# Two graph attention layers: V of layer 0 in two halves, second half of a step reordered, a PSUM copy split over two engines

## The chip, the cores and the metric

The kernel runs on one core of a Trainium2 chip. The metric is the device time of one execution in microseconds (us). Before the change it was 3313.61 us (median of 3 runs, 3313.41 to 3314.32). All runs told of here were in the fast state. PE is TensorE, DVE VectorE, ACT ScalarE, POOL GpSimd; PEld is TensorE's weight load.

## The reference, cut to what matters

`x` is 128 graphs of 128 nodes by 512 features, `adj` their masks. Two attention layers, each with a residual and a layer norm; all in float32.

```python
# layer 0: 4 heads of 64
sim = where(adj, (x@Wq)(x@Wk)^T / 8, -max)
x = layernorm(x + softmax(sim) @ (x@Wv) @ Wo + bo)
# layer 1: 8 heads of 64, its own layer norm first, the diagonal added to the mask
q, k, v = split((layernorm(x)*gamma + beta) @ w_qkv.T)
scores = where(adj | eye, q k^T / 8, -1e9)
x = layernorm(x + softmax(scores) @ v @ w_out.T + b_out)
```

## The kernel before

Graphs go in groups of two. The program is a pipeline written by hand: step `s` makes Q, K and V of layer 0 for group s, layer 0's attention for group s-1, layer 1's projections for group s-2 (seven half-size products instead of eight, `p("qk", i)` and `p("v", i)`) and layer 1's attention for group s-3. There are 67 steps (0 to 66); each has two halves, one for each graph of the group. The order of issue in the program is the order on each engine.

```python
def p(kind, *which, g=s - 2):
    for i in which:
        product(kind, g, i)
    if setup:                 # preparatory work: layer 1's weights, gamma and beta transposed (17 pieces),
        setup.pop(0)()        # then weight_sums: 16 subtractions on VectorE
k = 2 * s
scores(k); c(0); flush(); residual(0, k - 1); p("", g=-1); c(1); flush(); p("", g=-1)
normalised(k); residual(1, k - 1); p("v", 4, 3, g=s - 3); flush()
transposed(1, s - 2); probs_t(k); p("qk", 1, 2); attend(k); load(s + 2); p("", g=-1)
k += 1                        # the second half
scores(k)
p("qk", 6, 5)
flush()
residual(0, k - 1)
p("qk", 7)
c(2)                          # V of layer 0, both graphs: 16 matmul passes
flush()
normalised(k)
residual(1, k - 1)
p("qk", 4, 3)
flush()
probs_t(k)
p("v", 1, 2)
attend(k)
p("v", 6, 5, 7)
transposed(0, s + 1)
```

(The calls of the first half are set on fewer lines here.) What they do:

- `scores`: TensorE makes q k^T of both layers into two PSUM tiles (sc); GpSimd fills sm, VectorE copies the scores in under the mask and reduces the maxima; the exponentials (ScalarE) are put in a list, which `flush` issues.
- `normalised`: VectorE takes the reciprocal sums (rec), GpSimd multiplies: `sm = sm * rec`, 128x512 for layer 0, 128x1024 for layer 1.
- `probs_t`: TensorE transposes sm into PSUM (pt); ScalarE copies layer 0's, VectorE layer 1's (pT).
- `attend`: TensorE makes V^T P^T (av), ScalarE copies it (aT), and for layer 1 scales the layer norm's output (h); GpSimd adds the bias.
- `residual(l, ...)`: TensorE multiplies by the output weights (o), VectorE adds and takes the statistics (st, mv), GpSimd makes 1/std (ve, rstd); the norm itself (VectorE) goes on the list.

The PSUM tiles of scores, pt and av (two banks each) share two buffers; the other results share two one-bank buffers; layer 1's products have two accumulators, "a" and "f".

## Time and profile before

| | before |
|---|---|
| time, median | 3313.61 us |
| profile's span | 3310.9 us |
| TensorE busy | 99% |
| VectorE, ScalarE, GpSimd busy | 47%, 40%, 41% |
| a step, scores to scores | 50.81 us |

The page's first part gives busy time and share for each engine. The chain of waits goes back from the last instruction to what released each one; where it names TensorE all along, only that engine's own work and what interrupts it count. The lines themselves are in the prediction.

### The profile page before, as it was taken

The numbers are of one execution on the slowest core, as the hardware profiler recorded it, in microseconds if no ns is written. First come the engines' busy times: TensorE is split into PE (matmuls) and PEld (weight loads), VectorE is DVE, ScalarE is ACT, GpSimd is POOL, SyncE is SP. The second block draws the span as 40 slices with busy tenths as digits, with TensorE's granted clock in tenths as the row PEclk, the third lists the DMA queues.
The fourth block names the chain that finished last, engine by engine and source line by source line (L and its number), as shares of the span: only waits on it lengthen the run. The fifth ranks groups of instructions, "written<-read, shape, count | busy, mean of one in ns | idle before, by whom it ended". The sixth has DMA issues, their size and how long they took to land.

```text
span 3310.9 us, 56223 instructions
## 1 busy us (share of the span) xinstructions
PE 3261.8 (99%) x22337; PEld 2650.8 (80%) x22337; DVE 1560.4 (47%) x2840; ACT 1330.8 (40%) x4432; POOL 1354.6 (41%) x1799
## 2 busy tenths in 40 slices
PE   8999999999999999999999999999999999999997
PEld 6888788888888887888888878888888788888875
DVE  3444444444544454445444444454444444444453
ACT  3444334434444343344443433443444344434443
POOL 2434444344344444443444444434434444344343
PEclk9999999999999999999999999999999999999998
DMA  3000000000000000000000000000000000000000
GB/s 117 21 17 24 17 27 24 17 24 27 17 24 21 24 24 17 26 25 17 24 26 19 24 17 27 24 18 24 27 17 24 17 27 24 17 24 27 11 13 17
DMA packets 57976, 79.64 MB, mean 24 GB/s; under 512 B 20840, under 2 KB 22384, under 8 KB 57712
## 3 DMA queue, kind: packets, MB, share of 16 engines
q1 hardware_dynamic: 57712, 76.04, 7.1%
q8 instruction: 175, 2.87, 0.4%
q14 instruction: 89, 0.73, 0.1%
HBM read 42.47 MB, written 33.55 MB: 23 GB/s over the span
## 4 chain that ended last, share of the span: by engine, by line
PE 96%; ACT 2%; DVE 1%; POOL 1%; issue 0%; DMA 0%; SPq 0%; POOLq 0%; DVEq 0%; ACTq 0%
PE o L411 19%; PE qka L233 14%; PE p L283 14%; PE va L233 7%; PE qkf L233 7%; PE p L293 7%; PE av L388 6%; PE sc L322 5%; PE pt L366 5%; PE qkc L233 3%; PE xt L178 3%; PE vf L233 3%; PE vc L233 2%; ACT aT L393 2%; POOL sm L356 0%
## 5 line engine op out<-in xcount | busy, mean ns | idle before, releaser
L347 ACT ACTIVATE sm<-sm,nmax 128x128 f32<-128x128 f32 x1536 | 595.2, 389 | 471.7 <-DVE nmax L338 469.7
L411 PE MATMUL o<-wo,aT 128*128 128x512 f32 x1536 | 704.3, 595 | 0.7 <-ACT aT L393 0.7
L411 PEld LDWEIGHTS o<-wo,aT 128*128 128x128 f32 x1536 | 287.6, 191 | 258.8 <-issue 247.9
L424 POOL TENSOR_SCALAR ve<-mv 128x1 f32<-128x1 f32 x256 | 56.9, 222 | 1044.3 <-DVE mv L421 1044.0
L356 POOL TENSOR_TENSOR sm<-sm,rec 128x512 f32<-128x512 f32 (+1 forms) x256 | 370.9, 1470 | 254.0 <-DVE rec L355 251.4
L283 PE MATMUL p<-xT,w 128*128 128x256 f32 x2048 | 472.2, 384 | 2.3 <-ACT xT L180 1.2
L283 PEld LDWEIGHTS p<-xT,w 128*128 128x128 f32 x2048 | 385.3, 191 | 87.5 <-issue 28.7
L335 DVE COPY_PREDICATED sm<-m,sc 128x512 f32<-128x512 uint8 (+1 forms) x512 | 271.5, 583 | 319.1 <-POOL sm L333 255.7
L402 POOL TENSOR_TENSOR h<-h,bias 128x512 f32<-128x512 f32 x128 | 162.1, 1266 | 506.1 <-ACT h L401 506.1
L347 ACT ACTIVATION_READ_ACCUMULATOR sm<-sm,nmax 128x1 f32 x1536 | 286.6, 187 | 0.0
L233 PEld LDWEIGHTS qka<-xs,wsqk 128*128 128x128 f32 x2048 | 243.2, 191 | 38.1 <-issue 27.5
L233 PE MATMUL qka<-xs,wsqk 128*128 128x128 f32 x2048 | 256.0, 278 | 0.0
L233 PE MATMUL qkf<-xs,w 128*128 128x128 f32 x2048 | 249.6, 275 | 0.0
L338 DVE TENSOR_REDUCE nmax<-sm 128x4 f32<-128x512 f32 (+1 forms) x256 | 243.9, 953 | 8.8
L417 DVE TENSOR_TENSOR y<-o,h 128x512 f32<-128x512 f32 x128 | 88.3, 690 | 324.9 <-PE o L411 324.9
L322 PE MATMUL sc<-qk 64*128 64x128 f32 x3072 | 224.6, 286 | 15.6 <-ACT aT L393 15.6
L233 PEld LDWEIGHTS qkf<-xs,w 128*128 128x128 f32 x2048 | 239.0, 192 | 0.0
L293 PE MATMUL p<-w,xT 128*128 128x256 f32 x1024 | 231.7, 379 | 0.2 <-DVE h L417 0.2
L322 PEld LDWEIGHTS sc<-qk 64*128 64x128 f32 x3072 | 187.4, 188 | 50.7 <-ACT aT L393 27.5
L393 ACT COPY aT<-av 128x768 f32<-128x768 f32 (+2 forms) x132 | 102.9, 780 | 302.8 <-PE av L388 302.8
L293 PEld LDWEIGHTS p<-w,xT 128*128 128x128 f32 x1024 | 189.7, 190 | 23.6 <-DVE h L417 0.4
L366 PE MATMUL pt<-ident,sm 128*128 128x128 f32 x1536 | 190.9, 274 | 12.6 <-POOL sm L356 12.6
(86 smaller groups left out, 4775.6 us busy)
## 6 DMA issues: line engine op xcount, KB each, us to landing
x<-in_x_dram SPq DMA_DIRECT2D x64, 512.0 KB, 3.7
out_dram<-y SPq DMA_DIRECT2D x128, 256.0 KB, 2.1
w_qkv<-in_L_gnn_w_qkv_dram SPq DMA_DIRECT2D x12, 256.0 KB, 5.6
m<-in_adj_dram SPq DMA_DIRECT2D x64, 32.0 KB, 3.5
w_out<-in_L_gnn_w_out_dram SPq DMA_DIRECT2D x4, 256.0 KB, 4.2
w<-in_L_gnn_Wq_dram SPq DMA_DIRECT2D x1, 512.0 KB, 4.4
w<-in_L_gnn_Wk_dram SPq DMA_DIRECT2D x1, 512.0 KB, 6.2
w<-in_L_gnn_Wv_dram SPq DMA_DIRECT2D x1, 512.0 KB, 7.1
```

The lines of the kernel that those rows point to most:

```text
L233: nc.tensor.matmul(o, lhsT, rhs, start=first and n == 0, stop=n == len(todo) - 1, skip_group_check=True)
L283: nc.tensor.matmul(pm[:, (f % 2) * T:(f % 2 + 1) * T], W[l][:, c, f * P:(f + 1) * P], xT[:, c, :], start=(c == 0), stop=(c == KC - 1))
L293: nc.tensor.matmul(pm[:, (b - b0) * I:(b - b0 + 1) * I], xT[:, c, b * N:(b + 1) * N], W[l][:, c, 2 * I:3 * I], start=(c == 0), stop=(c == ...
L322: nc.tensor.matmul(ps[:, h % 2, h // 2, :], qk[r, h // 2, t], qk[r, H_ // 2 + h // 2, t], start=True, stop=True)
L335: nc.vector.copy_predicated(sm[:, s], mask[:, None, :].to_broadcast([P, K, N]), ps[:, s, :K, :])
L338: nc.vector.tensor_reduce(nmax, sm, AX.X, ALU.max, negate=True)
L347: nc.scalar.activation(sm[:, s, k, :], sm[:, s, k, :], AF.Exp, bias=nmax[:, s, k:k + 1], accum_out=total[:, s, k:k + 1])
L356: nc.gpsimd.tensor_tensor(sm, sm, rec[:, :, :, None].to_broadcast([P, 2, K, N]), op=ALU.mult)
L366: nc.tensor.transpose(pt[:, j, :], sm[:, j, :], ident)
L388: nc.tensor.matmul(pm[s * D:(s + 1) * D, at + kk * N:at + (kk + 1) * N], v[:, b, h * D:(h + 1) * D], pT[:, s * K + kk, :], start=True, sto ...
L393: nc.scalar.copy(aT[:, lo - base:hi - base], pm[:, lo:hi])
L411: nc.tensor.matmul(pm, aT[:, c * P:(c + 1) * P], WO[l][:, c, :], start=(c == 0), stop=(c == nk - 1))
```

## The change

Its intent: put TensorE work (half of V) between the second scores and the attention ahead of them, so that the scores don't wait for aT; spread layer 1's products more finely; and share the copy of layer 1's transposed probabilities between two engines.

```diff
         else:
-            per = 512 // I
-            b0 = (n - nq) * per
-            for b in range(b0, b0 + per):
-                for c in range(KC):
-                    nc.tensor.matmul(pm[:, (b - b0) * I:(b - b0 + 1) * I], ...
-            dst = V[l, g][:, b0:b0 + per, :]
+            b = n - nq
+            for c in range(KC):
+                nc.tensor.matmul(pm[:, :I], xT[:, c, b * N:(b + 1) * N], W[l][:, c, 2 * I:3 * I], ...
+            dst, src = V[l, g][:, b, :], pm[:, :I]
...
             else:
-                nc.vector.tensor_copy(pT, pt[:, :H_, :])
+                nc.scalar.copy(pT[:, :K], pt[:, :K, :])
+                nc.vector.tensor_copy(pT[:, K:], pt[:, K:, :])
...
         load(s + 2)
+        c(2)
         p("", g=-1)
...
         p("qk", 7)
-        c(2)
         flush()
+        residual(1, k - 1)
         normalised(k)
-        residual(1, k - 1)
-        p("qk", 4, 3)
+        p("qk", 4)
         flush()
+        p("qk", 3)
+        p("v", 1)
         probs_t(k)
-        p("v", 1, 2)
+        p("v", 2)
+        c(3)
         attend(k)
```

(cut at the "..." inside the calls and between the hunks)

More of the change, by code (lines that the diff above doesn't have):

```diff
@@ L288, in chunk @@
         else:
-            per = 512 // I
-            b0 = (n - nq) * per
-            for b in range(b0, b0 + per):
-                for c in range(KC):
-                    nc.tensor.matmul(pm[:, (b - b0) * I:(b - b0 + 1) * I],
-                                     xT[:, c, b * N:(b + 1) * N], W[l][:, c, 2 * I:3 * I],
-                                     start=(c == 0), stop=(c == KC - 1))
-            dst = V[l, g][:, b0:b0 + per, :]
-            src = pm.rearrange("p (b i) -> p b i", i=I)
+            b = n - nq
+            for c in range(KC):
+                nc.tensor.matmul(pm[:, :I], xT[:, c, b * N:(b + 1) * N], W[l][:, c, 2 * I:3 * I],
+                                 start=(c == 0), stop=(c == KC - 1))
+            dst, src = V[l, g][:, b, :], pm[:, :I]
         if (n + l) % 2:
```

## The prediction

> **What bounds the kernel now.** I read the page first (busy shares and the chain of waits), then that chain in order of time for a stretch in the middle, then the timelines of VectorE, GpSimd and ScalarE for the same stretch.
>
> ```profile
> span 3310.9 us, 56223 instructions
> PE 3261.8 (99%) x22337; PEld 2650.8 (80%) x22337; DVE 1560.4 (47%) x2840; ACT 1330.8 (40%) x4432; POOL 1354.6 (41%) x1799
> PE 96%; ACT 2%; DVE 1%; POOL 1%; issue 0%; DMA 0%; SPq 0%; POOLq 0%; DVEq 0%; ACTq 0%
> ```
>
> TensorE is busy for 99% and carries 96% of the chain; no other engine is over 47%. So only what stops TensorE counts. Here is one half of a step in the chain (start, length, what):
>
> ```profile
> 1535.80 1.49 PE av L388 x24
> 1537.28 0.02 issue
> 1537.30 0.81 ACT aT L393
> 1538.11 0.04 issue
> 1538.15 1.16 PE sc L322 x16
> 1539.32 1.98 PE qka L233 x16
> 1541.30 1.79 PE qkf L233 x16
> 1543.09 1.72 PE o L411 x4
> 1544.80 1.78 PE qka L233 x16
> 1546.59 3.46 PE p L293 x16
> 1550.04 3.43 PE o L411 x8
> 1553.48 1.78 PE qka L233 x16
> 1555.26 1.79 PE qkf L233 x16
> 1557.05 1.31 PE pt L366 x12
> 1558.36 0.87 PE va L233 x4
> ```
>
> A step takes 50.81 us (first scores at 1514.52 and again at 1565.33 in the chain), and in these two steps the only piece that is not TensorE's is the ScalarE copy aT. After the first half's attention (av) the scores of layer 1 need the PSUM buffer that av holds, so they wait for aT. From the end of av (1537.28) to the end of the scores (1539.32) is 2.04 us; in the first half, with work in between, the same 24 score matmuls take 1.54 us in the chain. **The stall is 0.50 us a step**, and the wait table has it 62 times ("PE sc <- ACT aT").
>
> The second thing to read is slack. The probabilities' transposes (pt) need GpSimd's multiplication by the reciprocal sums:
>
> ```profile
> 1551.46 2.89 POOL L356 TENSOR_TENSOR sm<-sm,rec 128x512 f32<-128x512 f32 x2 [3.11 <-DVE rec L355]
> 1555.24 0.22 POOL L424 TENSOR_SCALAR ve<-mv 128x1 f32<-128x1 f32 x1 [0.89 <-DVE mv L421]
> 1555.55 0.58 POOL L431 TENSOR_TENSOR rstd<-ve,mhalf 128x1 f32<-128x1 f32 x1
> 1556.10 1.27 POOL L402 TENSOR_TENSOR x<-x,bias 128x512 f32<-128x512 f32 x1
> ```
>
> The pair of multiplications (layer 0, then layer 1) ends at 1554.35 and pt runs from 1557.05: 2.7 us of slack, today. In the second half the order is: multiplications, then residual(1)'s variance and power (ve, rstd). The change swaps them.
>
> **What the Trainium skill says.** "TensorEngine Tiling (Array Packing)", Key Properties: changing the tiling mode drains TensorE. The trace agrees: scores use 64 rows and av 64 columns, and the product after each is 0.20 us longer than its like (in the chain p after sc 3.65 against 3.45, va after av 1.06 against 0.86). "TensorE: Matmul & The Clock Gate", the table at its top: ScalarE, VectorE and GpSimd are strict FIFO; the trace's order on each is the program's, so the swap above binds. "Advanced Engine Details and Errata", Bank Collisions: ScalarE and VectorE may read PSUM at once if their banks differ; the split copy of pT does that, and no trace of before has this pair to judge. "GPSIMD Engine Reference", Specifications: its SBUF interface is contended by VectorE instructions with two SBUF inputs. The x bias add is 1264 to 1707 ns by its line, median 1268, so lengthening is rare.
>
> **The change, part by part.**
>
> (a) V of layer 0, batch 0, moves between av and the second scores; batch 1 moves to just before the second av. The 16 matmuls (3.46 us) become 8 and 8, 1.73 each. The first 8 follow av directly, so they pay the switch: 1.93. They cover aT's 0.81 and the scores fall to 1.54. Sum before: 2.04 + 3.46 = 5.50. After: 1.93 + 1.54 + 1.73 = 5.20 (the switch into and out of the second av is there already). **Gain 0.30 us a step**: 0.50 of stall less 0.20 for one more switch. The evictions are one 128x512 VectorE copy (691 ns) replaced by a 128x256 on VectorE (about 424, the like-sized v adds) and one on ScalarE (about 372, the v copies); both beside TensorE work.
>
> (b) pT of layer 1: 1224 ns on VectorE become about 691 on VectorE and 586 on ScalarE in parallel. av waits for pT 2.8 us in the whole run, so nearly nothing is gained here: some 0.5 us for each of the last two half-steps, where the chain does run through this copy.
>
> (c) The second half's order. Between o (layer 1) and pt TensorE now has qk4, qk3 and one v product: 1.78 + 1.79 + 0.87 = 4.44 us (before 3.57). But the multiplications, which used to start during o, now follow residual(1), which needs o's end. Count from the first matmul of o (1549.88 in TensorE's timeline; the chain books it from 1550.04, the end of the piece before). VectorE's add started at 1553.52, 3.64 after; the statistics ended at 1555.15; ve started 5.36 after and GpSimd was free again at 1556.10, 6.22 after. These depend only on o, as VectorE's earlier queue (layer 0's norms) is done some 2 us after o starts. So the multiplications run from 6.22 to 6.22 + 2.89 = 9.11 (layer 0's 1040 ns end at 7.26, layer 1's 1897 ns at 9.11). TensorE without a wait: o ends 3.60 after (1553.48), and 4.44 more bring it to pt at 8.04; layer 0's four transposes are in time, and all twelve would end at 9.35. Layer 1's eight cannot start before 9.11 + 0.04; the chain shows once, near the end, what such a wait looks like:
>
> ```profile
> 3199.41 2.89 POOL sm L356 x2
> 3202.29 0.04 issue
> 3202.34 1.09 PE pt L366 x8
> ```
>
> So 0.04 from GpSimd's end, then 1.09 for the eight: they end at 9.11 + 0.04 + 1.09 = 10.24, against 9.35. **New stall 0.89 us a step**, which nothing later gives back: TensorE's order is fixed and it is the bound.
>
> Sum: +0.89 - 0.30 = +0.59 us a step. Both layers are present in 61 steps (3 to 63 of 0 to 66): +36.0. Step 64 has no V to fill in, so +0.9; step 65 has layer 1 alone, 8 transposes without the four ahead and one multiplication: about +0.4; the last step gains about 1.0 by (b); the three first steps pay the switch or lose nothing, +0.4. Together about +36.7: 3313.6 + 36.7 = **3350 us**.
>
> **Rivals.**
> - *The transposes don't stall*: then only (a) counts, 61 x -0.30 = -18, 3295 us. For it: the change was surely meant so, and first-half slack is large (multiplications end 2.8 us ahead of pt). Against it: the sums in (c) leave minus 0.8 us, and each is a duration in the trace.
> - *The stall is longer*: norms and multiplications now run on VectorE and GpSimd at once. GpSimd's tiny ratio op takes 340 to 606 ns, the longer ones beside VectorE's norms. Another 0.3 to 0.5 us on the multiplications would make +55 to +67, 3368 to 3381 us. But layer 1's multiplications have a mean of 1897 ns and a longest of 1900, although those of the second half already run beside VectorE's residual add.
> - *aT's wait is replaced, not removed*: the scores' masks wait for GpSimd's memset (VectorE idles 3.97 before it), which hangs on av's end and not on the scores. It moves 1.9 us towards the scores' start, so it only relaxes; a fresh PSUM wait for the half chunks is unlikely, since each evicted tile is over 1 us old when it is needed. If it held, (a) would give 0 and the time would be near 3369.
>
> **Range and chances.** The mechanism of (c) carries the sign. I give it about 85%. With it the stall is 0.7 to 1.2 us, so 3338 to 3369; without it about 3295. Range 3328 to 3370. Two per cent are 66 us: slower by more needs 1.1 us a step net, about twice the sum; 6%. Faster by over 2% would need all switches gone too; 1%.
>
> **What would show it.** In the changed chain: sc after the V half in 1.54 with no aT ahead of it (a); a POOL sm piece ahead of "PE pt x8" in every second half, of about 0.9 us, with the eight at 1.09 (c); in the wait table "PE pt <- POOL sm" some 62 times in place of "PE sc <- ACT aT"; GpSimd's rstd ahead of sm in the second half; a period of 51.4 us. I am wrong if pt runs x12 in 1.31 in the second half, or if the multiplications there start before ve.

## The result, and the profile after

The changed kernel took **3373.82 us** (4 runs, 3372.97 to 3374.29), beside 3313.97 for the kernel before: +59.9 us, ratio 1.018 (95% interval 1.0162 to 1.0197). A ratio is the mean time of one kernel's fast runs over that of the other's of the same rounds, so it isn't quite the ratio of the medians quoted. The predicted 3350 and its range to 3370 were too low.

The page of the changed kernel, the lines that answer to the first ones in the prediction:

```profile
span 3372.1 us, 56347 instructions
...
PE 3274.9 (97%) x22337; PEld 2638.5 (78%) x22337; DVE 1518.3 (45%) x2840; ACT 1423.6 (42%) x4624; POOL 1374.7 (41%) x1799
...
PE 86%; POOL 7%; DVE 4%; issue 1%; ACT 1%; DMA 0%; SPq 0%; POOLq 0%; DVEq 0%; ACTq 0%
```

TensorE's share of the chain fell from 96 to 86%, and GpSimd and VectorE came in with 7 and 4. The chain in order of time (start, length, what) shows where, in one half step of the middle:

```profile
1519.00 1.92 PE p L291 x8
1520.92 1.54 PE sc L318 x24
...
1529.73 3.45 PE o L408 x8
...
1533.93 0.71 DVE st L416
...
1534.93 0.21 POOL ve L421
...
1535.77 3.08 POOL sm L352 x2
...
1538.89 1.09 PE pt L362 x8
```

The scores are back at 1.54 us with no aT ahead of them, after V's half in 1.92. But behind o the chain leaves TensorE, goes through the residual's statistics and GpSimd's ve and sm, and comes back at the transposes. In TensorE's own timeline the twelve transposes, start to the start of what follows, take 2.38 us in this half against 1.31 before: a stall of 1.07 us in each step. The step, scores to scores, is 51.56 us.

Two timelines of the next step show something that I had only among the rivals, first GpSimd's and then VectorE's (start, length, instruction):

```profile
1587.33 3.08 POOL L352 TENSOR_TENSOR sm<-sm,rec 128x512 f32<-128x512 f32 x2
```
```profile
1587.40 1.26 DVE L439 TENSOR_SCALAR y<-y,mv,rstd 128x512 f32<-128x512 f32 x1 [0.84 <-POOL rstd L428]
```

The norm on VectorE now runs at the same time as the multiplications. It takes 1.26 us where it takes 0.55 alone, and the pair of multiplications takes 3.08 where it took 2.89. Of the pair, the one that the norm meets, layer 0's, keeps its 1.04 us (1587.33 to 1588.37), and the norm ends 0.28 us after it. Layer 1's, next in GpSimd's queue, is the one that grows, from 1.90 us to 2.08:

```profile
1588.32 2.08 POOL L352 TENSOR_TENSOR sm<-sm,rec 128x1024 f32<-128x1024 f32 x1
```

The wait table (engine and tile, what it waited for; us in all, times, longest):

```profile
DVE pT L368 <- ACT pT L367: 307.1, 127, 4.4
...
PEld pt L362 <- POOL sm L352: 96.4, 71, 14.3
```

The second line is the new stall. The first says that VectorE's half of pT waits for ScalarE's half nearly every time: the two copies don't run together at all.

Last, the start. The chain of the changed kernel in step 1:

```profile
49.31 0.61 DVE wsqk L153
...
57.87 0.06 DVE wsv L156
...
58.21 0.70 DVE h L414
```

From 49.3 to 57.9 us VectorE does nothing but the 16 weight sums, and the residual's add (h), the reciprocals of the exponentials' sums and the transposes stand behind them. In the kernel before they were issued two calls of `p` later. VectorE's timeline there:

```profile
50.78 0.17 DVE L355 RECIPROCAL rec<-total 128x4 f32<-128x4 f32 x1
50.87 0.66 DVE L153 TENSOR_TENSOR wsqk<-w 128x512 f32<-128x512 f32 x1
```

There they come behind the reciprocals, that is after all that the transposes needed. From the scores of step 1 to those of step 2 (starts in TensorE's timeline) it is 26.8 us before and 37.4 after.

### The profile page after: what moved, and what is told of

It is laid out like the page before. It is cut to its first block, busy times and chain, and to the rows that moved or that the text cites. A ratio compares the mean times of both kernels' runs of the same rounds, so it can differ in the third digit from the quotient of the medians.

```text
span 3372.1 us, 56347 instructions
## 1 busy us (share of the span) xinstructions
PE 3274.9 (97%) x22337; PEld 2638.5 (78%) x22337; DVE 1518.3 (45%) x2840; ACT 1423.6 (42%) x4624; POOL 1374.7 (41%) x1799
## 4 chain that ended last, share of the span: by engine, by line
PE 86%; POOL 7%; DVE 4%; issue 1%; ACT 1%; DMA 0%; SPq 0%; POOLq 0%; DVEq 0%; ACTq 0%
PE o L408 19%; PE p L283 13%; PE qka L233 10%; PE p L291 7%; POOL sm L352 6%; PE sc L318 6%; PE av L385 6%; PE va L233 5%; PE pt L362 5%; PE qkf L233 3%; PE qkc L233 3%; PE xt L178 3%; PE vf L233 3%; PE vc L233 2%; DVE st L416 1%
## 5 line engine op out<-in xcount | busy, mean ns | idle before, releaser
L352 POOL TENSOR_TENSOR sm<-sm,rec 128x512 f32<-128x512 f32 (+1 forms) x256 | 382.2, 1514 | 49.7 <-DVE rec L351 47.1
L362 PE MATMUL pt<-ident,sm 128*128 128x128 f32 x1536 | 205.9, 277 | 78.1 <-POOL sm L352 78.0
L233 PEld LDWEIGHTS qka<-xs,wsqk 128*128 128x128 f32 x2048 | 243.4, 192 | 37.9 <-issue 30.1
L362 PEld LDWEIGHTS pt<-ident,sm 128*128 128x128 f32 x1536 | 174.1, 142 | 102.8 <-POOL sm L352 96.4
L291 PE MATMUL p<-w,xT 128*128 128x256 f32 x1024 | 249.9, 387 | 0.2 <-ACT w L117 0.2
L368 DVE COPY pT<-pt 128x512 f32<-128x512 f32 x128 | 88.5, 692 | 307.1 <-ACT pT L367 307.1
```

The source lines that it names most:

```text
L233: nc.tensor.matmul(o, lhsT, rhs, start=first and n == 0, stop=n == len(todo) - 1, skip_group_check=True)
L291: nc.tensor.matmul(pm[:, :I], xT[:, c, b * N:(b + 1) * N], W[l][:, c, 2 * I:3 * I], start=(c == 0), stop=(c == KC - 1))
L352: nc.gpsimd.tensor_tensor(sm, sm, rec[:, :, :, None].to_broadcast([P, 2, K, N]), op=ALU.mult)
L362: nc.tensor.transpose(pt[:, j, :], sm[:, j, :], ident)
```

## The experiments

Twelve kernels ran, all with correct results. Each is given against the kernel before of its own rounds: 3315.3 us for the first four, 3315.2 for the second four, 3314.4 for the last. "Period" is the step in the middle, scores to scores in TensorE's timeline. There is no e9: that kernel was built and not run, and the record has nothing of it.

### The two causes, one at a time

**e1_no_swap**: the changed kernel with the swap undone.

```diff
-        residual(1, k - 1)
         normalised(k)
+        residual(1, k - 1)
         p("qk", 4)
```

> The changed kernel with one thing undone: in the second half the multiplications by the reciprocal sums are again issued before residual(1). My theory (the swap makes the new stall at the transposes, 1.07 us a step in the changed kernel's trace): the stall goes in all steps, the period falls from 51.56 to about 50.49 us, the time from 3373.8 by some 62 x 1.07 = 66 to about 3307 us; the 12 us that the start of the changed kernel is longer stay. Rival (the transposes come too early because V's matmuls no longer lie ahead of them, whatever the order of the multiplications): a stall of at least 0.5 us a step stays and the time is over 3335.

Measured: 3308.35 us, ratio 0.9979 (0.9971 to 0.9988), period 50.49; all twelve transposes in 1.31 us. The stall is the swap's, and nothing of it stays. Step 1 is still 37.9 us.

**e2_old_setup**: the changed kernel with preparatory work at ten pieces a step; the two new calls `p("qk", 4)` and `p("v", 1)` take none.

```diff
-            if setup:
+            if setup and pop:
```

> The changed kernel, but the pieces of preparatory work (transposes of layer 1's weights, then their sums on VectorE) are taken at the old pace, ten a step instead of twelve. Theory: the changed kernel's start is 12 us longer because VectorE's 16 weight sums (about 9 us) now come directly behind the second scores of step 1, ahead of the residual's add; at the old pace step 1 is 26 to 28 us again and not 37.4, the period stays 51.56, and the time falls by 10 to 12 to about 3362 us. Rival (the start is longer because V of layer 0 is made in two halves, each with its own PSUM tile): within 3 us of 3374.

Measured: 3365.03 us, ratio 1.0149, period 51.57; step 1 takes 28.4 us instead of 37.4. It is the place of the weight sums: here they come behind the reciprocals again, and the chain of step 1 has none of them. Splitting `p("qk", 4, 3)` and `p("v", 1, 2)` into more calls looked like a finer mixing of products, but every call also takes a piece of preparatory work. Some 1.6 us of step 1 and 1.0 ahead of it stay over the kernel before. Of the 1.6, V's halves alone bring 1.2 (e4: step 1 takes 28.0 us). The 1.0 can't be told from chance: e5, e8, e10, e11 and e13 issue the same program as the kernel before up to the scores of step 1, and reach them, partly on other chips, 0.6 to 3.4 us later than its profile does.

**e3_no_swap_old_setup**: both.

> Both undone together: V's halves, the split copy of the probabilities and the finer mixing of products stay. Theory: the two causes are separate and add up: 3373.8 - 66 - 12 = about 3296 us, period 50.49. Rival (they overlap, or the rest of the change costs something too): 3305 to 3325 us.

Measured: 3295.92 us, ratio 0.9942 (0.9928 to 0.9957), period 50.49, step 1 28.6 us. The causes add up: e1 took off 65.5 us and e2 8.8, both together 77.9. Of the 3.6 between, 3.0 lie in the profiles ahead of the scores of step 1, where nothing can be told from chance (see e2); that 3296 was met to the microsecond is luck, since e2 alone had fallen short of its 10 to 12.

**e4_v_only**: the kernel before with V's halves alone.

```diff
+        c(2)                  # behind load(s + 2), ahead of the second scores
...
-        c(2)                  # behind p("qk", 7)
...
         p("v", 1, 2)
+        c(3)
         attend(k)
```

> The kernel before with part (a) alone: V of batch 0 between attention and the second scores, V of batch 1 before the second attention. Theory: 0.30 to 0.32 us a step less, 61 steps: 3314 - 19 = about 3295 us, period 50.49, no wait of the scores for aT. Rival (the split copy or the reordered products carry part of the gain): over 3303 us, and slower than the changed kernel with swap and pace undone.

Measured: 3297.14 us, ratio 0.9946 (0.993 to 0.9963), period 50.49. Its interval overlaps that of e3 almost wholly: the split copy and the mixing bring nothing that the runs can see in the total. Part (a) is worth 0.32 us a step, 0.30 predicted.

**e5_swap_only**: the kernel before with the swap alone (the same two lines as e1, the other way round).

> The kernel before with the swap alone: in the second half residual(1) ahead of the multiplications. Theory: the multiplications then end some 9.3 us after the first matmul of o, as in the changed kernel, but no v product stands between the second products and the transposes, which would have ended at 3.60 + 1.78 + 1.79 + 1.31 = 8.48; with 0.04 and 1.09 they end at 10.43. So the stall is 1.95 us a step, 0.87 more than in the changed kernel, the period about 52.76, and the time 3314 + 119 + a few at the end = about 3436 us. Rival (the stall belongs to the new places of V and not to the swap): within 20 us of 3314.

Measured: 3424.6 us, ratio 1.0331 (1.0316 to 1.0346), period 52.57. The swap alone costs 1.75 us a step, and more here than in the changed kernel, as the missing v product says. It is 0.20 less than I expected, and the trace tells why. Here the norms are issued behind product 3, and a norm starts only when layer 1's multiplication, the second of the pair, already runs (1607.17 to 1609.06 us). VectorE's timeline:

```profile
1607.79 1.55 DVE L442 TENSOR_SCALAR y<-y,mv,rstd 128x512 f32<-128x512 f32 x1
```

The norm is longer still, and again ends 0.28 us after the multiplication that it met. But no multiplication is next in turn, and the pair takes 2.90 us. I had carried over the 3.08 of the changed kernel. 1.95 less 0.19 is 1.76.

### What lengthens the multiplications

**e6_norms_late**: the changed kernel with layer 1's norms behind the transposes.

```diff
         p("qk", 4)
-        flush()
         p("qk", 3)
         p("v", 1)
         probs_t(k)
+        flush()
```

> The changed kernel, with layer 1's norms on VectorE issued behind the probabilities' transposes and their copies instead of ahead of qk 3. Theory: GpSimd's pair of multiplications takes 3.08 us in the changed kernel against 2.89 before because the norms run at the same time (they themselves take 1.26 us there against 0.54); without them the pair is back at 2.89, the stall 0.89 as predicted, the period 51.37 and the time 3373.8 - 12 = about 3362 us. Rival (VectorE's add of the qk products lengthens them, which still runs beside them): 3.08 again, and 3374 us.

Measured: 3363.6 us, ratio 1.0147 (1.0132 to 1.0162), period 51.38. GpSimd's and VectorE's timelines:

```profile
1582.00 2.90 POOL L352 TENSOR_TENSOR sm<-sm,rec 128x512 f32<-128x512 f32 x2
```
```profile
1587.30 0.54 DVE L439 TENSOR_SCALAR y<-y,mv,rstd 128x512 f32<-128x512 f32 x1
```

Apart from each other, both are at their old lengths, and the stall is 0.89 us (transposes in 2.20 against 1.31), the size predicted. The add of the qk products (1583.01 to 1583.70 in the same timeline) still runs beside the multiplications and costs them nothing.

### The split copy

**e7_two_tiles**: the changed kernel with ScalarE's and VectorE's halves of pT in two SBUF tiles.

```diff
-                nc.scalar.copy(pT[:, :K], pt[:, :K, :])
-                nc.vector.tensor_copy(pT[:, K:], pt[:, K:, :])
+                nc.scalar.copy(pA, pt[:, :K, :])
+                nc.vector.tensor_copy(pB, pt[:, K:, :])
```

> The changed kernel with the transposed probabilities of layer 1 in two tiles, one for each engine. In the changed kernel VectorE's half waits for ScalarE's half in 127 of 128 cases, 307 us in all, so the two do not run in parallel as I had predicted. Theory: the wait is there because both write one tile, and goes with two tiles; the copies then overlap; since the copies are off TensorE's path in the middle of the run the period stays 51.56, and only the last half-steps gain, about 0.7 us for each of two or three: 3371 to 3374 us. Rival (the wait is for reading the same PSUM tile): the wait stays and nothing changes.

Measured: 3374.36 us, ratio 1.018, period 51.56. My theory fell: VectorE's copy still starts when ScalarE's has ended. The output tile isn't the reason.

**e12_single_banks**: the changed kernel with one-bank PSUM tiles; pT is one tile again, aT is two copies.

```diff
-        return ps_at.tile([P, 2, 512], F32, tag="at", name=name)
+        return [ps_at.tile([P, 512], F32, tag="at", bufs=4, name=f"{name}_{i}") for i in range(2)]
...
-                nc.vector.tensor_copy(pT[:, K:], pt[:, K:, :])
+                nc.vector.tensor_copy(pT[:, K:], pt[1])
...
-        nc.scalar.copy(aT[:, lo - base:hi - base], pm[:, lo:hi])
+        for l, g, b in both:
+            lo, hi = (base, 512) if l == 0 else (512, 1024)
+            nc.scalar.copy(aT[:, lo - base:hi - base], pm[l][:, lo - 512 * l:hi - 512 * l])
```

> The changed kernel with its two-bank PSUM tiles made as two tiles of one bank each (four buffers); aT is then two copies. With two tiles of probabilities in SBUF, VectorE's copy still waited for ScalarE's, so the output tile isn't the reason. Theory: both engines read one PSUM tile and the program orders that; with a tile for each bank the wait of VectorE's copy for ScalarE's (about 307 us in all) goes and the two copies overlap as I had predicted; the time stays within 6 us of 3374, as the copies are off TensorE's path, or falls a little at the end. Rival (ScalarE and VectorE don't read PSUM together in this place): the wait stays.

Measured: 3364.03 us, ratio 1.0149 (1.0134 to 1.0165), period 51.44. VectorE's and ScalarE's timelines:

```profile
1562.54 0.69 DVE L368 COPY pT<-pt 128x512 f32<-128x512 f32 x1 [0.72 <-PE pt L362]
```
```profile
1563.07 0.62 ACT L367 COPY pT<-pt 128x512 f32<-128x512 f32 x1
```

Now they overlap, by 0.16 us here, and VectorE waits for TensorE only. So it was the PSUM tile shared by two readers that the program put in order, although each reads its own bank. The time fell more than I expected, by 10 us, and 7 of these have nothing to do with pT: layer 0's part of aT is copied while av still runs, so ScalarE reaches v's product 6 earlier, and product 7, which waited 0.12 us for that copy, doesn't wait any more (0.12 x 61 = 7). The other 3 are in the last three steps (0.5, 0.6 and 1.9 us); which of the copies brings them was not taken apart.

### A cheaper way to the same gain

**e8_scores_order**: the kernel before; in the second half TensorE makes layer 1's scores first.

```diff
-        for l, g, b in both:
+        for l, g, b in both[::-1] if k % 2 else both:
...
+        if k % 2:
+            made.reverse()
```

> Another way to the same gain: the kernel before, in which TensorE makes the scores of layer 1 ahead of those of layer 0 in the second half. The first takes the PSUM buffer that is free, and its 16 matmuls (1.03 us) cover the copy aT (0.85 us with its hand-over) that the second one's buffer waits for. Theory: the stall of 0.50 to 0.52 us goes without the extra change of tiling mode that V's halves cost: period 50.29 to 50.33, time 3314 - 61 x 0.5 = about 3283 us. Rival (VectorE, which now gets layer 0's scores 1 us later, delays the softmax until the transposes wait): over 3300 us.

Measured: 3307.44 us, ratio 0.9977 (0.9969 to 0.9985), period 50.69. The stall at the scores went (24 in 1.61), but three quarters of the gain did not arrive. The chain, and ScalarE's timeline:

```profile
1542.62 1.72 PE o L413 x4
...
1544.41 2.02 PE qka L233 x16
```
```profile
1543.71 0.56 ACT L259 COPY eqk<-qka 128x512 f32<-128x512 f32 x1
```

Product 7 (qka) adds into the accumulator from which ScalarE has first to copy product 6 (eqk). That copy stands behind layer 0's exponentials, which hang on the end of av over aT, h, the bias, the memset and the masks, and so do not come earlier when the scores do. TensorE, 0.45 us earlier than before, runs into it and loses 0.32. In the kernel before, the stall at the scores had hidden this wait.

**e10_copy_first**: the same, with the copy of product 6 ahead of the exponentials.

```diff
-        flush(1)
+        if k % 2 == 0:
+            flush(1)
```

> Layer 1's scores first had removed the stall at the scores (24 in 1.61 us), but gained 0.13 us a step and not 0.5: product 7 now waits 0.32 us for ScalarE's copy of product 6 (both use one PSUM accumulator), and that copy stands behind layer 0's exponentials. This kernel issues the copy of product 6 ahead of the exponentials. Theory: the copy is then done right after product 6, the wait goes, the period is 50.685 - 0.32 = about 50.37 us and the time 3314 - 61 x 0.45 = about 3287 us. Rival (the whole second half hangs on the chain from av's end over aT, the layer norm's scale, the bias, the memset and the masks to the exponentials, so another wait appears): over 3298 us.

Measured: 3287.82 us, ratio 0.9919 (0.9904 to 0.9934), period 50.37, as the theory said.

**e11_scale_late**: with, besides, ScalarE's scale of h behind the copy of v's product 6 in the second half.

```diff
-        p("v", 6, 5, 7)
+        product("v", s - 2, 6)
+        scaled()              # h's scale and bias of both layers' inputs, taken out of attend
+        p("v", 5, 7)
```

> The same, and in the second half ScalarE's scale of the layer norm's output (0.72 us) is issued behind the copy of v's product 6 instead of ahead of it. v's product 7 waits for that copy in every step (62 waits in the kernel before). Theory: product 5 then covers the copy, v's products 5 and 7 lose their 0.02 and about 0.10 us, period about 50.25, time some 7 us under the run with the copy of product 6 first: about 3280 us. Rival (the 0.10 us behind v's product 7 is not from this wait): within 3 us of that run.

Measured: **3280.31 us**, ratio 0.9896 (0.9881 to 0.9911), period 50.24. v's products 5 and 7 take 0.86 us each. It beats both kernels: 34 us under the one before, of the same rounds, and 93.5 under the changed one.

**e13_av_last**: e10 with the second attention directly ahead of the next scores.

```diff
-        attend(k)
         p("v", 6, 5, 7)
         transposed(0, s + 1)
+        attend(k)
```

> The kernel with the copy of product 6 first, and the second attention moved behind v's products and x's transposes, directly ahead of the next step's scores, which also take layer 1 first. Theory: one change of tiling mode less (0.20 us a step) and no wait of v's product 7 (0.12): period about 50.05 us, 3287 - 19 = about 3268 us. Rival (the chain from av over aT, scale, bias and memset to the masks, 3.3 us, now delays the first half's softmax by about 2.6 us against 2.8 us of slack at its transposes, and other waits come in): a stall at the first half's transposes and a period of 50.4 us or more.

Measured: 3380.23 us, ratio 1.0197 (1.018 to 1.0214). The rival was right in its chain and wrong in its place. The chain of waits:

```profile
1543.81 0.47 POOL sm L334
...
1548.69 0.61 DVE qk L301
...
1549.35 3.72 PE p L283 x16
```

VectorE's copy of the first Q and K chunk stands behind the delayed masks and maxima, and TensorE needs its PSUM buffer two tiles later; the transposes themselves were in time. I had looked at the slack of one consumer of VectorE and not at the others in its queue.

## Why the prediction was right or wrong

By the spans of the profiles the change cost 61.2 us, where 36.7 were summed up. The start up to the scores of step 1 is read in the chains (30.02 and 31.42), the later steps as starts of the scores; the last row is what is left. Of the 24.5 us that the sum missed, 12.0 lie in the first steps, 9.6 in the middle and 2.9 at the end.

| term | predicted | measured |
|---|---|---|
| steps 0 to 2 | +0.4 | +12.4 (1.4 to the first scores, 10.6 in step 1, 0.4 in step 2) |
| steps 3 to 63 | 61 x 0.59 = +36.0 | +45.6 (0.75 a step) |
| last steps | +0.3 | +3.2 |

- **The bound, and part (a): right.** The wait for aT was the only one in the step, V's half cost one more change of tiling mode, from av's 64 columns back to 128 (1.92 us for the 8 passes, 1.93 predicted), and e4 measures the gain alone at 0.32 us.
- **Part (c), mechanism: right.** The multiplications behind residual(1) make layer 1's eight transposes wait, by the chain as written: e1 takes the stall away by the swap alone, e5 makes it by the swap alone.
- **Part (c), size: too small.** The term mis-sized is "6.22 + 2.89 = 9.11". The pair measured 3.08, and the stall 1.07 instead of 0.89. Over 61 steps the 0.18 are 11 us. I had this among the rivals and set it aside because layer 1's multiplications were 1900 ns at most even beside VectorE's residual add. But that add reads PSUM and one SBUF tensor. The norm is the operation that newly falls beside them. One hint of what it does was the small ratio operation (340 against about 600 ns beside a norm), which I named and gave little weight. Another lay in step 1 of the kernel before, which I hadn't looked at: beside VectorE's weight sums, which read two SBUF tensors, a multiplication takes 1.39 us instead of 1.04 and the bias add 1.71 instead of 1.27, and two of the sums take 1.41 and 1.64 instead of 0.69.

  The Trainium skill has this contention, on a page that I hadn't read: "SBUF — State Buffer", Who interferes with whom, names `tensor_scalar` among the VectorE operations that can contend with GpSimd for a shared pair of ports, and says that who issues first has it for the whole instruction. The row that the prediction cites from "GPSIMD Engine Reference" names, besides two SBUF inputs, a two-port mode of VectorE, and the prediction left that out. The runs agree on the pair of operations: together 1.26 and 3.08 us, apart 0.54 and 2.90 (e6). They agree on who waits, too: 62 norms of the changed kernel and 63 of e5 start inside a multiplication and end 0.28 us after it (median), and the multiplication keeps its length, 1.04 or 1.90. Whether the norm runs in that mode, and which port it is, no run shows.
- **The start: wrong.** The step that failed is "the three first steps pay the switch or lose nothing, +0.4". I compared what each engine computes in a step and did not count what `p` does besides. With twelve calls a step instead of ten, the 18 pieces of preparatory work end in the sixth call of step 1 and no longer in its eighth, and the weight sums land ahead of the residual and the softmax. e2 gives back 9 us of step 1. The 1.4 us up to the first scores are within what the start varies by (see e2).
- **Part (b): wrong, and nearly without weight.** "In parallel" failed: the program orders two readers of one PSUM tile (e7 and e12). The predicted gain of 1.0 us in the last step did not come: from the last reduction of the maxima in the chain to the end it is 24.4 us in both kernels. In e12, where the copies overlap, the last step is 1.2 us shorter than in the kernel before; aT's two copies may have a part in that.
- **Of the rivals**, "the transposes don't stall" fell by the trace, and "aT's wait is replaced, not removed" did not come true for this change, since V's half lies ahead of the scores. It did come true for e8, by the accumulator and not by the memset. The measured time lies in the band of "the stall is longer" (3368 to 3381), but by luck: its mechanism is right and worth 11 us, not 18 to 30, and the start brought the rest.

What stays open: the +3.2 us of the last steps are 1.2 in step 64, 1.2 in step 65 and 0.7 in the last. Without the swap (e1) 2.6 of them go. The other 0.6 are not there with V's halves alone (e4); whether the split copy or the mixing brings them is not known.

## What to carry to other kernels

When TensorE is at 99%, a reorder is worth what it does to the slack of every chain that comes back to it: write down for each consumer when its input is ready, counted from the same TensorE instruction, and do it again for whatever newly runs at the same time. A wait that is removed lets the engine arrive earlier at the next one; e8 gained only when the next wait was removed too. And before judging a regrouping of calls as neutral, read what else the helper does on each call: here a counter of calls decided where 9 us of VectorE work landed.

## What the Trainium skill lacked or had wrong

- "TensorEngine Tiling (Array Packing)", Key Properties, says that a change of tiling mode drains TensorE and gives no size: here 0.20 us for an excursion into another mode and back (va after av 1.06 against 0.86 us).
- "GPSIMD Engine Reference", Specifications, names the conditions of contention with VectorE but no size, and "SBUF — State Buffer", Who interferes with whom, gives two ratios without their operations. Here a norm that starts inside a multiplication takes 1.26 or 1.55 us instead of 0.54 and ends 0.28 us after it. That the first one keeps its length agrees with the page (1.04 and 1.90). What no page has is a size for these waits, or for the loss of the instruction next in turn: layer 1's multiplication, 2.08 instead of 1.90. With VectorE's weight sums, which read two SBUF tensors, both sides were lengthened (1.39 instead of 1.04 and 1.41 instead of 0.69).
- "Advanced Engine Details and Errata", Bank Collisions, says that ScalarE and VectorE may read different PSUM banks at once; e12 agrees (0.62 and 0.69 us, overlapping by 0.16). No page that I read says that a program may still order them when both banks are one tile: 307 us of waits in the changed kernel, none of that kind in e12.
